# The queries' product between scores and sums, feed-forward products interleaved, and PSUM banks from a list

## The chip, the core and the metric

The kernel runs on one core of one Trainium2 chip. The metric is device microseconds of one execution. The core has TensorE (PE; its weight loads are shown apart as PEld), VectorE (DVE), ScalarE (ACT), GpSimd (POOL) and SyncE (SP), which issues the DMAs. TensorE writes to PSUM, 8 banks of 512 float32 per partition; VectorE and ScalarE read it from there.

## What is computed

A layer over `x` of shape (2, 256, 128, 128): batch, times T, bands FB, channels C. In float32, with 4 heads of 32 channels:

```python
xt = _ln(x, ln_t_w, ln_t_b).transpose(0, 2, 1, 3)
x = x + _mha(xt, t_wi, t_bi, t_wo, t_bo, H_T, causal mask over 256 times).transpose(0, 2, 1, 3)
xf = _ln(x, ln_f_w, ln_f_b)
x = x + _mha(xf, f_wi, f_bi, f_wo, f_bo, H_F, mask of the bands within 16 of each other)
xn = _ln(x, ln_n_w, ln_n_b)
h = gelu(xn @ w1.T + b1)          # 512 hidden channels
x = x + (h @ w2.T + b2)
```

`_mha` is attention: queries, keys and values from one product each, scores, softmax, weighted values, and an output product.

## The kernel before

**Groups.** The work is cut into 384 groups of 512 tokens (4 tiles of 128): 128 groups of attention over time (`OverTime`), and then, in 16 runs of 8 + 8, 128 groups of attention over bands (`OverBands`) and 128 of feed-forward (`FeedForward`). A run's 8 groups of bands are followed by the 8 feed-forward groups of the same tokens.

**The order is written out by hand.** `run` (line 1275) loops over n, and in iteration n it issues steps of several groups: the scores or first hidden products of group n, the sums of group n-1, the output of group n-2, queries, keys and values of group n+1, the normalization of group n+3. Every engine is wrapped by `InOrder` (line 897), so that each engine does its instructions in exactly that order. All recorded instructions therefore carry line 907, and groups are told apart by tile names.

**One group over bands, as TensorE meets it in iteration n** (8 groups of a run; when all neighbours are groups over bands):
- `first_half` / `scores` (775, 810): 64 matmuls from `qT`, `kT` into 4 banks, in 32x64 tiles of the array;
- `weigh` (814) of group n-1: the sums `rp` (`pf` by ones) and the weighted values `op` (`pf` by `v`), in 128x32 tiles;
- `output` (630) of group n-2: `wn` by `oT`;
- `queries_keys` (571) and `values` (590) of group n+1: `xnT` by `wf`, 128x32 tiles again. `product` (646) makes 4 matmuls, one for each 32 columns of the array; each stands as two records in the profile.

ScalarE in the same iteration: 4 exponentials (`first_function`, 790), `invert` (602) of group n-1, that is the logarithm `ln` of the sums and the exponential `r`, then the copies `qT`, `kT` and `v` of group n+1 out of PSUM.

VectorE: the band bias on the fourth head's scores (`bank<-bank,band`), `normalize` (441) of group n+3 (`xh`), `turn` (458), a transpose into `z`, `finish` (636) of group n-2, which adds the output product to the stream (`x<-bank`), `divide` (615) of group n-1 in three steps (`bank<-bank,r`, `u`, `oT`), and from the fifth group of a run on the statistics of a later group (`stats`, `mv`).

SyncE writes `z` to DRAM in four DMAs (`turned`), and `fetch` (470) reads the turned tile back as `xnT`, one iteration later, for the group two ahead of the iteration.

**One feed-forward group**: `first_half` (855) makes two of the four hidden products from `xnT`, `first_function` their gelus; then `weigh` (869) of group n-1 multiplies the hidden tile `hT` by `w2T` (16 products of 128 columns); then `second_half` and `second_function` the other two hidden products and gelus; `divide` (886) adds the result to the stream (`res`). In the first feed-forward group of a run (`turn`), the last group over bands is inverted by one VectorE `reciprocal` (`invert_exactly`, 610), and its output product comes at the end of the next iteration (line 1439).

**Banks.** `bank` (947) hands out PSUM banks: in the stage over time by fixed places, and in the other stages by counting round eight (`turn_of_bank`, 943); `follow` and `held` (line 817) set aside the turns of the output and of the next queries before the sums take theirs. A product into a bank waits until its last reader is done.

Of the kernel before, what the change touches and what calls it, by code (L numbers as in the profile page):

```python
# [19 lines left out]
P = 128  # L20
H = 4
# [4 lines left out]
NT = 4  # L26
# [343 lines left out]
class Group:  # L370
# [7 lines left out]
    def __init__(self, path, src, dst, before=None, store=None):  # L378
        self.path, self.src, self.dst = path, src, dst
        self.before, self.store = before, store  # L380

# [179 lines left out]
class Attention(Group):  # L561
    which = None
    swapped = ()
# [7 lines left out]
    def queries_keys(self):  # L571
        path = self.path
        wf = path.k.wf[self.which]
        self.qp = path.bank([P, NT * P], "qp", self.place.get("qp", path.held.pop("qp", None)))
        product(path, self.qp, wf[:, 0:P], self.xnT)

        self.kp = path.bank([P, NT * P], "kp", self.place.get("kp"))
        product(path, self.kp, wf[:, P : 2 * P], self.xnT)

    def take_query(self):  # L580
        path = self.path
        self.qT = path.work.tile([P, NT * P], F32, name="qT")
        path.scalar.activation(self.qT, self.qp, AF.Identity, bias=path.k.bq[self.which], scale=1.0)

    def take_key(self):
        path = self.path
        self.kT = path.work.tile([P, NT * P], F32, name="kT")
        path.scalar.copy(self.kT, self.kp)

    def values(self):  # L590
        path = self.path
        wv = path.k.wf[self.which][:, 2 * P : 3 * P]
        self.vp = path.bank([P, NT, P], "vp", self.place.get("vp"))
        for i in range(NT):
            product(path, self.vp[:, i], self.xnT[:, i * P : (i + 1) * P], wv, turn=2 if i in self.swapped else 0)

    def take_values(self):
        path = self.path
        self.v = path.work.tile([P, NT, P], F32, name="v", bufs=4)
        path.scalar.copy(self.v, self.vp)  # L600

# [13 lines left out]
    def divide(self):  # L615

        path, vector = self.path, self.path.vector
        if self.r0 is None:
            self.oT = path.work.tile([P, NT * P], F32, name="oT", bufs=2)
            u = path.work.tile([P, NT * P], F32, name="u", bufs=2)  # L620
            vector.tensor_tensor(by_rows(u), by_tile(self.op), by_tile(self.r), ALU.mult)
            vector.tensor_scalar(self.oT, u, -1.0, None, ALU.mult)
            return
# [4 lines left out]
        vector.tensor_tensor(by_rows(self.oT), by_tile(self.op), by_tile(u), ALU.mult)  # L628

    def output(self):  # L630
        path = self.path
        self.yp = path.bank([P, NT, P], "yp", self.place.get("yp", path.held.pop("yp", None)))
        for i in range(NT):
            product(path, self.yp[:, i], self.oT[:, i * P : (i + 1) * P], path.k.wn[self.which])

    def finish(self):
        self.path.vector.tensor_tensor(self.dst(), self.yp, self.dst(), ALU.add)
        if self.store is not None:
            self.store()
# [13 lines left out]
class OverTime(Attention):  # L653
# [7 lines left out]
    def values(self):  # L661
        path = self.path
        wv = path.k.wf[self.which][:, 2 * P : 3 * P]
        self.vp = [path.bank([P, 2, P], "vp", self.place.get(f"vp{s}")) for s in range(2)]
        for i in range(NT):
            product(
                path, self.vp[i // 2][:, i % 2], self.xnT[:, i * P : (i + 1) * P], wv, turn=2 if i in self.swapped else 0
            )

    def take_values(self):  # L670
        path = self.path
        self.v = path.work.tile([P, NT, P], F32, name="v", bufs=4)
        for s in range(2):
            path.scalar.copy(self.v[:, 2 * s : 2 * s + 2], self.vp[s])

    def first_tiles(self):
        path = self.path

        self.p0 = path.work.tile([P, 2, H, 2 * P], F32, name="p0", tag="p", bufs=3)
        self.s0 = {h: path.bank([P, 2, 2 * P], "sp", path.banks[f"a{h}"]) for h in range(H)}  # L680

    def second_tiles(self):
        path = self.path

        self.p1 = path.work.tile([P, 2, H, 2, P], F32, name="p1", tag="h", bufs=2)
        self.s1 = {h: path.bank([P, 2, P], "sp", path.banks[f"b{h}"]) for h in range(H)}
# [15 lines left out]
    def first_weights(self, heads):  # L702
        for h in heads:
            self.path.scalar.activation(self.p0[:, :, h], self.s0[h], AF.Exp)

    def second_weights(self, heads):
        for h in heads:
            self.path.scalar.activation(self.p1[:, :, h, 0], self.s1[h], AF.Exp)

# [17 lines left out]
    def weigh(self):  # L727
        path, v = self.path, self.v
        rp = path.bank([P, 2, 2, P], "rp", self.place.get("rp"))
# [4 lines left out]
        op = path.bank([P, 2, 2 * P], "op", self.place.get("op"))  # L734
# [33 lines left out]
class OverBands(Attention):  # L768
# [3 lines left out]
    follow = ("yp",)  # L772
    by_vector = 1

    def scores(self, heads):
        path = self.path
        self.sp = {h: path.bank([P, NT * P], "sp") for h in heads}
# [12 lines left out]
    def first_function(self):  # L790
        path = self.path
        for h in range(H - self.by_vector, H):
            sp = self.sp[h].rearrange("p (i q) -> p i q", i=NT)
            path.vector.scalar_tensor_tensor(
                sp, sp, LIMIT, path.band.unsqueeze(1).to_broadcast([P, NT, P]), ALU.min, ALU.add
            )
        for h in range(H):
            path.scalar.activation(self.p[:, h].rearrange("p i q -> p (i q)"), self.sp[h], AF.Exp)

# [14 lines left out]
    def weigh(self):  # L814
        path = self.path

        path.held = {name: path.turn_of_bank() for name in self.follow}
        self.rp = path.bank([P, NT * P], "rp")
# [5 lines left out]
        self.op = path.bank([P, NT * P], "op")  # L824
# [7 lines left out]
class FeedForward(Group):  # L832
# [8 lines left out]
    def hidden(self, js):  # L841
        path = self.path
        for j in js:
            self.hp[j] = path.bank([P, NT * P], "hp")
            product(path, self.hp[j], path.k.w1f[:, j * P : (j + 1) * P], self.xnT)

    def gelus(self, js):
        path = self.path
        for j in js:
# [3 lines left out]
            )  # L853

# [13 lines left out]

    def weigh(self):
        path, NI = self.path, self.path.k.NI  # L870
        if self.last:
            zp = [path.bank([P, P], "zp") for i in range(NT)]
        else:
            self.zp = path.bank([P, NT, P], "zp")
# [11 lines left out]
    def divide(self):  # L886
# [5 lines left out]
        else:  # L892
            self.path.vector.tensor_tensor(self.dst(), self.zp, self.dst(), ALU.add)
        self.store()
# [17 lines left out]
class BoundedPath:  # L912
    def __init__(self, ctx, tc, k):
# [6 lines left out]
        self.next_bank = 0  # L920
        self.inputs = 0
        self.held = {}
# [24 lines left out]
    def bank(self, shape, name, i=None):  # L947

        flat = self.ps[self.turn_of_bank() if i is None else i][:, 0 : math.prod(shape[1:])]
# [224 lines left out]
    def verdict(self):  # L1174

        vector, C = self.vector, P
        tp = self.bank([P, 6], "tp")
# [97 lines left out]
    def run(self, x, out):  # L1275
# [15 lines left out]
        for i in range(len(groups) - 2):  # L1291
            if at(i, OverBands) and at(i + 1, OverBands):
                groups[i].follow = ("yp", "qp")

# [18 lines left out]
        for n in range(len(groups) + 2):  # L1313
# [6 lines left out]
            if n + 4 in early:  # L1320
                do(n + 4, "root")
            do(n, "first_half", "first_function", "first_mask")
# [90 lines left out]
            if not turn:  # L1413
# [11 lines left out]
            do_at(n + 1, OverBands, "queries_keys", "take_query", "take_key")  # L1425
# [15 lines left out]
            do_at(n + 1, OverBands, "values", "take_values")  # L1441
            if old is not None or new is not None:
# [70 lines left out]
```

## Time and profile before

| | us |
|---|---|
| median of 3 runs | 2633.58 (2631.95 to 2634.81) |
| span of the profiled execution | 2631.9 |
| stage over time, to about | 930 |
| 16 runs of 8 + 8 groups, each about | 106 |

Busy time by engine, in stretches of the profiled execution (us; the count of instructions in brackets):

```profile
800.00:875.00 75.00, 75.00 (x2048) 52.20 (x2036) 63.56 (x188) 67.84 (x155) 69.31 (x65) 1.00 0.62 157
...
2000.00:2500.00 500.00, 499.81 (x13008) 362.56 (x13004) 411.17 (x1232) 301.79 (x496) 332.86 (x461) 1.00 0.49 123
```

The columns are the stretch, its length, the busy time of PE, PEld, DVE, ACT and POOL, then the granted TensorE clock (1.00 is full), the DMA engines' busy share and GB/s.

How to read a timeline row: start and length in us, engine, source line, operation, out<-in by tile names, the shapes (output<-inputs; for matmuls the tile of the array as rows*columns), how many instructions are merged in it, and in brackets the engine's idle time before it with what ended that. PEld rows are weight loads, which run beside matmuls. SPq rows are the issues of DMAs.

### The profile page before, as it was taken

The numbers are of one execution on the slowest core, as the hardware profiler recorded it, in microseconds if no ns is written. First come the engines' busy times: TensorE is split into PE (matmuls) and PEld (weight loads), VectorE is DVE, ScalarE is ACT, GpSimd is POOL, SyncE is SP. The second block draws the span as 40 slices with busy tenths as digits, with TensorE's granted clock in tenths as the row PEclk, the third lists the DMA queues.
The fourth block names the chain that finished last, engine by engine and source line by source line (L and its number), as shares of the span: only waits on it lengthen the run. The fifth ranks groups of instructions, "written<-read, shape, count | busy, mean of one in ns | idle before, by whom it ended". The sixth has DMA issues, their size and how long they took to land.

```text
span 2631.9 us, 156460 instructions
## 1 busy us (share of the span) xinstructions
PE 2617.8 (99%) x68688; PEld 1837.4 (70%) x68688; DVE 2140.8 (81%) x6410; ACT 1838.8 (70%) x3543; POOL 1958.6 (74%) x2311
## 2 busy tenths in 40 slices
PE   9999999999999999999999999999999999999999
PEld 6666666666766767666777776667676677777776
DVE  8888888888888887977878779788797797887974
ACT  7989988999899875564655746647557466475573
POOL 7999999999999987666667666665776666757762
PEclk9999999999999999999999999999999999999999
DMA  6656555565565454445454544554454445554543
GB/s 155 167 149 158 149 149 149 155 155 149 149 158 149 122 127 119 115 123 127 118 124 124 123 122 117 126 128 120 122 126 120 120 119 131 123 120 123 123 104 88
DMA packets 469797, 344.97 MB, mean 131 GB/s; under 512 B 43120, under 2 KB 404464, under 8 KB 469104
## 3 DMA queue, kind: packets, MB, share of 16 engines
q1 hardware_dynamic: 468408, 334.41, 50.5%
q8 instruction: 540, 8.85, 1.5%
q14 instruction: 153, 1.25, 0.2%
q10 hardware_dynamic: 696, 0.46, 0.1%
HBM read 167.98 MB, written 166.72 MB: 127 GB/s over the span
## 4 chain that ended last, share of the span: by engine, by line
PE 99%; DVE 0%; issue 0%; DMA 0%; ACT 0%; ACTq 0%; DVEq 0%
PE bank L907 99%; DMA x<-in_x 0%; DVE xh L907 0%; DVE bank L907 0%; DVE res L907 0%; DVE stats L907 0%; DVE oT L907 0%; DVE u L907 0%; DVE xnT L907 0%; ACTq L907 0%; ACT p L907 0%; DVE vy L907 0%; ACT lnv L907 0%; DVE mv L907 0%; ACT root L907 0%
## 5 line engine op out<-in xcount | busy, mean ns | idle before, releaser
L907 ACT ACTIVATE hT<-bank,b 128x512 f32<-128x512 f32 x512 | 348.1, 688 | 524.2 <-PE bank L907 483.2
L907 POOL TENSOR_SCALAR_AFFINE_SELECT pf<-pf 128x512 f32<-128x512 f32 x768 | 477.7, 637 | 185.3 <-ACT pf L907 159.1
L907 PEld LDWEIGHTS bank<-w2T_sb,hT 128*32 128x32 f32 x16384 | 467.4, 110 | 54.8 <-issue 29.0
L907 PE MATMUL bank<-xnT,wf 128*32 128x512 f32 x4096 | 492.4, 592 | 0.5 <-DVE xnT L907 0.5
L907 PE MATMUL bank<-xnT,w1f 128*32 128x512 f32 x4096 | 486.3, 592 | 0.2 <-issue 0.2
L907 PE MATMUL bank<-w2T_sb,hT 128*32 128x128 f32 x16384 | 482.8, 273 | 1.0 <-issue 1.0
L907 ACT ACTIVATE p<-bank 128x512 f32<-128x512 f32 (+1 forms) x1024 | 430.6, 494 | 62.9 <-PE bank L907 62.9
L907 DVE TENSOR_SCALAR xh<-x,mv,rstd 128x160 f32<-128x160 f32 (+1 forms) x1012 | 394.3, 432 | 59.7 <-POOL rstd L907 49.4
L907 POOL TENSOR_SCALAR_AFFINE_SELECT p<-p 128x1024 f32<-128x1024 f32 (+2 forms) x384 | 364.5, 949 | 57.5 <-ACT p L907 49.1
L907 PEld LDWEIGHTS bank<-wf,xnT 128*32 128x32 f32 x8192 | 243.3, 110 | 144.1 <-issue 101.6
L907 POOL TENSOR_TENSOR p<-p,p 128x512 f32<-128x512 f32 x256 | 324.6, 1291 | 10.6
L907 DVE BATCH_NORM_STATS2 stats<-x 128x6 f32<-128x128 f32 x1536 | 329.0, 276 | 3.4 <-DMA x<-in_x 3.4
L907 POOL TENSOR_SCALAR rstd<-mv 128x4 f32<-128x4 f32 x251 | 57.8, 230 | 361.7 <-DVE mv L907 360.5
L907 PEld LDWEIGHTS bank<-xnT,w1f 128*32 128x32 f32 x4096 | 183.6, 110 | 171.6 <-issue 109.6
L907 PE MATMUL bank<-qT,kT 32*64 32x80 f32 (+4 forms) x16384 | 302.0, 271 | 0.1
L907 PEld LDWEIGHTS bank<-qT,kT 32*64 32x64 f32 x16384 | 260.0, 131 | 51.2 <-ACT kT L907 50.6
L907 DVE TENSOR_TENSOR res<-bank,res 128x512 f32<-128x512 f32 (+1 forms) x259 | 170.3, 658 | 153.3 <-PE bank L907 144.7
L907 ACT ACTIVATE pf<-bank 128x512 f32<-128x512 f32 x512 | 265.8, 602 | 35.5 <-PE bank L907 31.3
L907 PE MATMUL bank<-wn,oT 128*32 128x128 f32 x8192 | 283.8, 274 | 0.1
L907 DVE STREAM_TRANSPOSE z<-xh 128x512 f32<-128x512 f32 x380 | 270.3, 711 | 13.3
L907 PE MATMUL bank<-wf,xnT 128*32 128x128 f32 x8192 | 276.5, 273 | 0.0
L907 POOL TENSOR_TENSOR rstd<-rstd,mhalf 128x4 f32<-128x4 f32 x251 | 260.8, 1039 | 20.9
(100 smaller groups left out, 3820.3 us busy)
## 6 DMA issues: line engine op xcount, KB each, us to landing
turned<-z SPq DMA_DIRECT2D x1520, 64.0 KB, 2.7
xnT<-turned SPq DMA_DIRECT2D x380, 256.0 KB, 3.2
x<-res SPq DMA_DIRECT2D x256, 128.0 KB, 2.5
x<-x SPq DMA_DIRECT2D x128, 256.0 KB, 4.1
out<-res SPq DMA_DIRECT2D x252, 128.0 KB, 2.3
x<-in_x SPq DMA_DIRECT2D x124, 256.0 KB, 4.3
x<-in_x SPq DMA_DIRECT2D x4, 128.0 KB, 2.8
x<-in_x SPq DMA_DIRECT2D x6, 64.0 KB, 2.9
```

The costliest lines, as they stand in the source:

```text
L907: return self.tc.keep_in_program_order(emit(*args, **kwargs))
```

## The change

1. `queries_keys` is split into `queries` and `keys`. Where groups n and n+1 are both over bands, the queries' product of group n+1 is issued between the scores of group n and the sums of group n-1, and its copy `take_query` behind `invert` (logarithm and `r`) of group n-1. Keys, their copy and values stay where they were. This concerns 7 of the 8 groups of a run.
2. Where groups n-1 and n are both feed-forward (7 iterations of a run), `weigh_around` issues tiles 0 and 1 of group n-1's second product, then hidden product 2 of group n, tiles 2 and 3, then hidden product 3. The gelus of products 2 and 3 follow.
3. Banks are taken from `free`, a list whose first entry has been free longest, and put back at its end once the last reader has been issued. In groups over bands that follow one another, the banks of sums and weighted values go back only at the end of the iteration (`keep`, `give_sums`). The stage over time keeps its fixed places.

```diff
+    def take(self, name, shape, i=None):
+        free = self.path.free
+        if i is None:
+            i = free[0]
+        if i in free:
+            free.remove(i)
+        self.taken[name] = i
+        return self.path.bank(shape, name, i)
+
+    def give(self, *names):
+        for name in names:
+            if name in self.taken:
+                self.path.release(self.taken.pop(name))
...
+    def weigh_around(self, other):
+        self.zp = self.take("zp", [P, NT, P])
+        self.weigh_tiles(range(0, 2))
+        other.hidden((2,))
+        self.weigh_tiles(range(2, NT))
+        other.hidden((3,))
...
-    def turn_of_bank(self):
-        i, self.next_bank = self.next_bank, (self.next_bank + 1) % 8
-        return i
...
+    def release(self, i):
+        if i in self.free:
+            self.free.remove(i)
+        self.free.append(i)
...
-            do(n - 1, "weigh")
+            if bands[2] and bands[3]:
+                do(n + 1, "queries")
+            if feeds[1] and feeds[2]:
+                groups[n - 1].weigh_around(groups[n])
+            else:
+                do(n - 1, "weigh")
             do(n - 1, "invert_exactly" if turn else "invert")
+            if bands[2] and bands[3]:
+                do(n + 1, "take_query")
             if new is not None:
                 new.first_weights(new.late)
             if bands[2] or turn:
                 do(n - 2, "output", "finish")
...
+            if bands[1] and bands[2]:
+                groups[n - 1].keep = True
             do(n - 1, "divide")
...
-            if not turn:
+            if feeds[1] and feeds[2]:
+                do(n, "second_function")
+            elif not turn:
                 do(n, "second_half", "second_function")
...
-            do_at(n + 1, OverBands, "queries_keys", "take_query", "take_key")
+            if bands[2] and bands[3]:
+                do(n + 1, "keys", "take_key")
+            else:
+                do_at(n + 1, OverBands, "queries_keys", "take_query", "take_key")
...
+            do_at(n - 1, OverBands, "give_sums")
```

`bands[i]` and `feeds[i]` tell whether group n-2+i is over bands or feed-forward, so `bands[2]` is group n itself.

More of the change, by code (lines that the diff above doesn't have):

```diff
@@ L569, in bias, with queries, keys, queries_keys @@
         )
-    def queries_keys(self):
+    def queries(self):
+        path = self.path
+        self.qp = self.take("qp", [P, NT * P], self.place.get("qp"))
+        product(path, self.qp, path.k.wf[self.which][:, 0:P], self.xnT)
+    def keys(self):
         path = self.path
         wf = path.k.wf[self.which]
-        self.qp = path.bank([P, NT * P], "qp", self.place.get("qp", path.held.pop("qp", None)))
-        product(path, self.qp, wf[:, 0:P], self.xnT)
-        self.kp = path.bank([P, NT * P], "kp", self.place.get("kp"))
+        self.kp = self.take("kp", [P, NT * P], self.place.get("kp"))
         product(path, self.kp, wf[:, P : 2 * P], self.xnT)
+    def queries_keys(self):
+        self.queries()
+        self.keys()
     def take_query(self):
@@ L592, in values @@
         wv = path.k.wf[self.which][:, 2 * P : 3 * P]
[L593 removed]
+        self.vp = self.take("vp", [P, NT, P], self.place.get("vp"))
         for i in range(NT):
@@ L628, in divide, with give_sums @@
         vector.tensor_tensor(by_rows(self.oT), by_tile(self.op), by_tile(u), ALU.mult)
+        if not self.keep:
+            self.give_sums()
+    def give_sums(self):
+        self.give("rp", "op")
     def output(self):
         path = self.path
-        self.yp = path.bank([P, NT, P], "yp", self.place.get("yp", path.held.pop("yp", None)))
+        self.yp = self.take("yp", [P, NT, P], self.place.get("yp"))
         for i in range(NT):
@@ L663, in values @@
         wv = path.k.wf[self.which][:, 2 * P : 3 * P]
-        self.vp = [path.bank([P, 2, P], "vp", self.place.get(f"vp{s}")) for s in range(2)]
+        self.vp = [self.take(f"vp{s}", [P, 2, P], self.place.get(f"vp{s}")) for s in range(2)]
         for i in range(NT):
@@ L679, in first_tiles @@
         self.p0 = path.work.tile([P, 2, H, 2 * P], F32, name="p0", tag="p", bufs=3)
-        self.s0 = {h: path.bank([P, 2, 2 * P], "sp", path.banks[f"a{h}"]) for h in range(H)}
+        self.s0 = {h: self.take(f"s0{h}", [P, 2, 2 * P], path.banks[f"a{h}"]) for h in range(H)}
     def second_tiles(self):
@@ L728, in weigh @@
         path, v = self.path, self.v
-        rp = path.bank([P, 2, 2, P], "rp", self.place.get("rp"))
+        rp = self.take("rp", [P, 2, 2, P], self.place.get("rp"))
         for n in range(2):
@@ L776, in scores @@
         path = self.path
-        self.sp = {h: path.bank([P, NT * P], "sp") for h in heads}
+        self.sp = {h: self.take(f"sp{h}", [P, NT * P]) for h in heads}
         for i in range(NT):
@@ L815, in weigh @@
         path = self.path
-        path.held = {name: path.turn_of_bank() for name in self.follow}
-        self.rp = path.bank([P, NT * P], "rp")
+        self.rp = self.take("rp", [P, NT * P])
         for h in range(H):
@@ L871, in weigh @@
         if self.last:
-            zp = [path.bank([P, P], "zp") for i in range(NT)]
+            zp = [self.take(f"zp{i}", [P, P]) for i in range(NT)]
         else:
-            self.zp = path.bank([P, NT, P], "zp")
+            self.zp = self.take("zp", [P, NT, P])
             zp = [self.zp[:, i] for i in range(NT)]
```

44 lines of the change are left out of this document (31 added, 13 removed).

## The prediction

> **What bounds the kernel now.** First the page: the span, the busy shares, the chain that ended last.
>
> ```profile
> span 2631.9 us, 156460 instructions
> PE 2617.8 (99%) x68688; PEld 1837.4 (70%) x68688; DVE 2140.8 (81%) x6410; ACT 1838.8 (70%) x3543; POOL 1958.6 (74%) x2311
> ...
> PE 99%; DVE 0%; issue 0%; DMA 0%; ACT 0%; ACTq 0%; DVEq 0%
> ```
>
> TensorE is busy all the way and the chain never leaves it. The ends of matmuls are modelled, so busy alone proves little. What settles it is whether matmuls start back to back, and that is read from the timeline by the distance from one start to the next. Here are TensorE's products in one group over bands, in the middle of a run of eight:
>
> ```profile
> 2432.03 0.97 PE L907 MATMUL bank<-qT,kT 32*64 32x80 f32 x64
> 2432.92 1.07 PE L907 MATMUL bank<-pf,ones 128*32 128x512 f32 x8
> 2433.80 1.06 PE L907 MATMUL bank<-pf,v 128*32 128x128 f32 x32
> 2434.68 1.06 PE L907 MATMUL bank<-wn,oT 128*32 128x128 f32 x32
> 2435.55 1.90 PE L907 MATMUL bank<-xnT,wf 128*32 128x512 f32 x16
> 2437.27 1.06 PE L907 MATMUL bank<-wf,xnT 128*32 128x128 f32 x32
> 2438.25 0.97 PE L907 MATMUL bank<-qT,kT 32*64 32x80 f32 x64
> ```
>
> From start to start: scores 0.89, sums 0.88, weighted values 0.88, output 0.87, queries and keys 1.72 (0.86 each), values 0.98, in all 6.22 us. The 32-column output and the values do the same work (32 matmuls of 128 columns), but values take 0.11 more because scores follow, in another tile shape. No product waits for data. So a reorder has almost nothing to win in such a group; what matters is whom the new order makes late.
>
> The engine nearest to being late is VectorE. Its timeline in the same place:
>
> ```profile
> 2433.18 0.70 DVE L907 SCALAR_TENSOR_TENSOR bank<-bank,band 128x512 f32<-128x512 f32 x1 [0.63 <-PE bank L907]
> ...
> 2435.42 0.71 DVE L907 STREAM_TRANSPOSE z<-xh 128x512 f32<-128x512 f32 x1
> 2436.06 0.65 DVE L907 TENSOR_TENSOR x<-bank,x 128x512 f32<-128x512 f32 x1
> 2436.64 0.69 DVE L907 TENSOR_TENSOR bank<-bank,r 128x512 f32<-128x512 f32 x1
> ...
> 2438.09 0.69 DVE L907 TENSOR_TENSOR oT<-bank,u 128x512 f32<-128x512 f32 x1
> 2438.69 0.86 DVE L907 BATCH_NORM_STATS2 stats<-x 128x6 f32<-128x128 f32 x4
> ...
> 2439.75 0.67 DVE L907 SCALAR_TENSOR_TENSOR bank<-bank,band 128x512 f32<-128x512 f32 x1
> ...
> 2446.29 0.67 DVE L907 SCALAR_TENSOR_TENSOR bank<-bank,band 128x512 f32<-128x512 f32 x1
> ...
> 2452.83 0.68 DVE L907 SCALAR_TENSOR_TENSOR bank<-bank,band 128x512 f32<-128x512 f32 x1
> ...
> 2458.32 0.69 DVE L907 SCALAR_TENSOR_TENSOR bank<-bank,band 128x512 f32<-128x512 f32 x1
> ```
>
> The row at 2433.18 (the fourth group's band bias) waited 0.63 for scores: VectorE still had time over. From the fifth group on it carries statistics too, and no later one of these rows shows idle time: they follow at 6.54 us (2439.75 to 2446.29 to 2452.83) where TensorE needs 6.22. VectorE falls behind by 0.3 a group. Where that lag ends is in the first feed-forward groups, where the last band group is inverted exactly:
>
> ```profile
> 2468.74 3.32 DVE L907 RECIPROCAL ln<-bank 128x512 f32<-128x512 f32 x1
> ...
> 2473.24 0.43 DVE L907 TENSOR_SCALAR oT<-u 128x512 f32<-128x512 f32 x1
> ```
> ```profile
> 2473.71 0.87 PEld L907 LDWEIGHTS bank<-wn,oT 128*32 128x32 f32 x30 [0.53 <-DVE oT L907]
> ```
> ```profile
> PEld bank L907 <- DVE oT L907: 9.9, 17, 0.8
> ```
>
> TensorE's output product of the last band group starts 0.04 after VectorE ends oT at 2473.67, and the table of waits counts 17 such: one for each of the 16 runs and one more. So at the end of every run it is VectorE's lag, not TensorE's own work, that says when TensorE goes on. What makes VectorE later between the fourth group and that point is paid in full, sixteen times.
>
> **The change part by part.** *Queries between scores and sums (7 of a run's 8 groups).* No instruction is added: TensorE's 6.22 us stay, and both neighbours have the sums' tile shape, so no switch is added. But sums, weighted values and the output product of two groups back each start 0.86 later. Behind the output product VectorE adds it to the stream (2436.06), and VectorE takes its work in program order: behind that add stand three steps of the division, the statistics and the next band bias. The output product now ends at 2435.55 + 0.86 = 2436.41. From the end of a product to VectorE's start the trace shows 0.26 (scores end at 2432.92, the band bias starts at 2433.18), so the add starts at 2436.67 instead of 2436.06: a new VectorE wait of 0.61. It arises in the third and in the fourth group. The third's is swallowed by the 0.63 that the fourth's band bias waits anyway; the fourth's is not, since nothing waits behind it any more. From the fifth group on VectorE's own lag hides the later product. So VectorE stands 0.6 later up to oT at 2473.24, and TensorE waits that much longer at 2473.71: 16 x 0.61 = 9.8 us. If VectorE had slack left there this would be 0; if the third group's wait passed through too, 19.5. I take 9.8, as the 0.63 is in the row.
>
> *Queries need their normalized input earlier.* The product moves ahead by sums, weighted values and output, 0.88 + 0.88 + 0.87 = 2.63 us. Its input comes by a DMA that SyncE issues when the transposed tile has landed.
>
> ```profile
> 2440.44 0.34 SPq L907 DMA_DIRECT2D xnT<-turned  x1
> ```
> ```profile
> DMA to landing us min/median/max: 2.6/3.2/4.9
> ```
> ```profile
> 1383.80 0.34 SPq L907 DMA_DIRECT2D xnT<-turned  x1
> ```
> ```profile
> 1386.07 1.06 PE L907 MATMUL bank<-pf,ones 128*32 128x512 f32 x8
> ...
> 1388.71 1.55 PE L907 MATMUL bank<-xnT,wf 128*32 128x512 f32 x12
> ```
>
> An ordinary fetch, issued at 2440.44 and landed by 2443.6 (median) or 2445.3 (worst), is wanted after the change behind the next group's scores, at 2438.25 + 6.22 + 0.89 = 2445.4: no wait, or just none. A late one, issued at 1383.80, is wanted at 1386.07 and lands at 1387.0 at the median, 1388.7 at worst: 0.9 to 2.6 of waiting. While TensorE waits there, sums and output stand behind it. Of the 16 runs a few have fetches like the second; my estimate from these rows is four late fetches a program of about 1 us, 4 us, with ends 0 and 9.
>
> *The queries' copy behind logarithm and reciprocal.* ScalarE's order is the same as before, only the copy's product is ready long before.
>
> ```profile
> 2454.66 0.63 ACT L907 ACTIVATE r<-ln 128x512 f32<-128x512 f32 x1
> 2455.48 0.69 ACT L907 ACTIVATE qT<-bank,bq 128x512 f32<-128x512 f32 x1 [0.19 <-PE bank L907]
> 2456.34 0.59 ACT L907 COPY kT<-bank 128x512 f32<-128x512 f32 x1 [0.17 <-PE bank L907]
> ```
> ```profile
> 2450.71 0.97 PE L907 MATMUL bank<-qT,kT 32*64 32x80 f32 x64
> ...
> 2457.09 0.97 PE L907 MATMUL bank<-qT,kT 32*64 32x80 f32 x64
> ```
>
> In the seventh group r ends at 2455.29, and the copies of queries and keys after it make scores late: 6.38 instead of 6.22. With the 0.19 before the queries' copy gone that is at most 0.16 a run, 2.6 us in all; but VectorE's extra 0.61 makes the exponentials, and so r, later again, and costs 0.2 to 0.5 there. Neither counts: TensorE catches up or not before 2473.71, where it waits for VectorE in any case. So 0, between -2.6 and +3.
>
> *Feed-forward products interleaved (7 of 8 groups).* Same products, same tile shape:
>
> ```profile
> L907 PE MATMUL bank<-xnT,w1f 128*32 128x512 f32 x4096 | 486.3, 592 | 0.2 <-issue 0.2
> L907 PE MATMUL bank<-w2T_sb,hT 128*32 128x128 f32 x16384 | 482.8, 273 | 1.0 <-issue 1.0
> ```
>
> Both stream 2,097,152 columns, and both take 483 to 486 us: a short product costs no more per column than a long one, so there is nothing to hide by mixing them. The Trainium skill ("TensorE: Matmul & The Clock Gate", back-to-back issue gap) says otherwise: about 81 ns for 128 columns and 131 ns for 512, that is, short products pay for their weight loads; by that rule mixing should gain. These rows do not show it here. The last gelu is covered by the next group's first two products (1.72 us against 0.69); the addition of the second product comes 0.86 later, on a VectorE that idles there once its lag is gone:
>
> ```profile
> 1547.49 0.69 DVE L907 TENSOR_TENSOR res<-bank,res 128x512 f32<-128x512 f32 x1 [2.02 <-PE bank L907]
> ```
>
> So 0; if the cover were missing, 0.86 in one group of a run, 14 us.
>
> *Banks by a list of freed ones.* Followed by hand, a list that gives the longest-freed bank gives in both stages the same distance as counting round eight. The tightest is scores on the bank of the output product: its add now ends near 2437.3 in the fourth group, scores start at 2438.25. So 0; up to 0.3 a group if VectorE's lag reaches it, which the 9.8 then contains.
>
> The sum: 9.8 + 4 = 13.8 on the profiled 2631.9 gives 2645.7. The profiled span is 1.7 below the median of the runs shown, 2633.6, so 2647.
>
> **Rivals.** *No change (24%).* VectorE's wait does not last: something in the 35 us between the fourth group and oT has slack that the timeline doesn't show, or the output product reaches VectorE sooner. For it: VectorE is busy only 81% over the span. Against it: the rows without idle time from 2439.75 on. Then 2633.6, down to 2631 with the seventh group's 2.6.
>
> *Faster (5%).* Weight loads do bound the short products. Then each group of the 112 interleaved ones has one more change from long to short, behind which one set of weight loads (110 ns, 467.4 us busy on the weight-load side over all short products) is hidden: 112 x 0.11 = 12.3, so 2621.
>
> ```profile
> L907 PEld LDWEIGHTS bank<-w2T_sb,hT 128*32 128x32 f32 x16384 | 467.4, 110 | 54.8 <-issue 29.0 <-ACT hT L907 10.9 <-ACT waste L907 0.3
> ```
>
> It decides from the point at which the first product behind a long one is cheaper than the others. The equal column rates speak against it. The Trainium skill's rule above (same page and section) is this mechanism stated for all kernels.
>
> *Slower still (7%).* The input is what binds: most of the 16 runs wait 1 us or more for a fetch, each wait holds back the output product and so VectorE again. 16 x (1 + 0.6) = 26 us, 2659. The decisive point is a fetch issued less than 3.2 us before the sums' old place.
>
> **How the numbers follow.** About 0.2% (5 us) can be told from no change. The forecast (64%) lies wholly above that, from +8 to +22. So slower 0.71, same 0.24, faster 0.05. The range 2631 to 2659 holds no change and the forecast with both its unknowns, and leaves out the faster rival and what is beyond the slower one. The forecast alone: 2641 to 2656.
>
> **What would show it.** In the changed timeline the add of the output should carry an idle time of about 0.6 before it in the third and fourth group of a run, ended by TensorE; the band biases after it should stand 0.6 further behind their scores; the wait of TensorE's weight loads for oT should grow from 9.9 to about 20 us. Some queries' products should start late behind scores, and the scores, feed-forward products and the stage over time should keep their distances. The prediction is wrong if the add shows no wait, or if it does and oT's wait doesn't grow.

## The result, and the profile after

| | us | against before |
|---|---|---|
| before, median of 6 runs beside it | 2633.94 (2631.95 to 2635.13) | |
| after, median of 6 runs | 2650.11 (2645.73 to 2660.39) | ratio 1.0066, 95% interval 1.0052 to 1.0079 |
| after, profiled execution | 2649.4, span 2646.7 | span 14.8 over before's 2631.9 |

The kernel became 16.2 us slower; 13.4 had been forecast. The page first: span, busy shares, and the chain that ended last.

```profile
span 2646.7 us, 156391 instructions
PE 2625.1 (99%) x68688; PEld 1872.6 (71%) x68688; DVE 2143.1 (81%) x6410; ACT 1835.2 (69%) x3543; POOL 1955.9 (74%) x2311
...
PE 92%; DMA 4%; DVE 3%; SPq 1%; issue 0%; ACT 0%; POOL 0%; ACTq 0%; DVEq 0%; POOLq 0%
```

Busy shares are as before; the chain is not. It had been TensorE for 99%, now 8% of it runs through DMA, VectorE and SyncE: TensorE waits for them in places.

Because all 16 runs of 8 + 8 groups are alike, the distance from one run's first scores to the next run's is the best measure in one trace. TensorE's timeline, before and after, the same run:

```profile
2413.32 0.96 PE L907 MATMUL bank<-qT,kT 32*64 32x80 f32 x64
...
2519.04 0.97 PE L907 MATMUL bank<-qT,kT 32*64 32x80 f32 x64
```
```profile
2426.60 0.97 PE L961 MATMUL bank<-qT,kT 32*64 32x80 f32 x64
...
2532.95 0.97 PE L961 MATMUL bank<-qT,kT 32*64 32x80 f32 x64
```

105.72 became 106.35. Of the 15 such distances in each trace, six before lie at 105.70 to 105.73 and seven after at 106.34 to 106.35: these are the undisturbed runs, and the change costs each of them 0.64 us. 16 x 0.64 = 10.2 of the 16.2. The other runs are longer by various amounts, in both kernels. Below, "shortest run" is that floor in a kernel's trace.

Where the 0.64 comes from is on VectorE. The additions of the output product (`x`) and the band biases, third to seventh group of that run:

```profile
2443.71 0.69 DVE L961 TENSOR_TENSOR x<-bank,x 128x512 f32<-128x512 f32 x1 [0.53 <-PE bank L961]
...
2446.39 0.70 DVE L961 SCALAR_TENSOR_TENSOR bank<-bank,band 128x512 f32<-128x512 f32 x1
...
2449.94 0.69 DVE L961 TENSOR_TENSOR x<-bank,x 128x512 f32<-128x512 f32 x1 [0.60 <-PE bank L961]
...
2453.66 0.67 DVE L961 SCALAR_TENSOR_TENSOR bank<-bank,band 128x512 f32<-128x512 f32 x1
...
2460.20 0.67 DVE L961 SCALAR_TENSOR_TENSOR bank<-bank,band 128x512 f32<-128x512 f32 x1
...
2466.74 0.67 DVE L961 SCALAR_TENSOR_TENSOR bank<-bank,band 128x512 f32<-128x512 f32 x1
```

The two additions in the third and fourth group wait 0.53 and 0.60 for TensorE; no later one does. The fourth group's band bias, idle for 0.63 before, has lost its slack. From there the biases follow at 6.54 as before, but each stands 0.63 further behind its scores.

Where TensorE pays for it is not where it was looked for. The table of waits, after, and the one row of it that is wanted of before:

```profile
DVE x L961 <- PE bank L961: 25.1, 36, 4.3
...
PEld bank L961 <- POOL pf L961: 15.7, 36, 0.9
...
PEld bank L961 <- DVE oT L961: 8.7, 16, 0.6
PE bank L961 <- DMA xnT<-turned: 8.5, 10, 1.9
```
```profile
PEld bank L907 <- POOL pf L907: 2.0, 8, 0.7
```

(Sum, count, longest.) VectorE's additions now wait 36 times, two a run and four more. The wait for `oT` has not grown from 9.9, it is 8.7. The wait for POOL's masks went from 2.0 to 15.7. POOL in the seventh group of a run, then TensorE's weight loads for the sums behind the eighth group's scores, after:

```profile
2573.55 0.23 POOL L961 TENSOR_SCALAR rstd<-mv 128x4 f32<-128x4 f32 x1 [1.29 <-DVE mv L961]
2573.86 1.04 POOL L961 TENSOR_TENSOR rstd<-rstd,mhalf 128x4 f32<-128x4 f32 x1
2574.87 5.22 POOL L961 TENSOR_SCALAR_AFFINE_SELECT pf<-pf 128x512 f32<-128x512 f32 x8
```
```profile
2578.85 0.11 PEld L961 LDWEIGHTS bank<-pf,ones 128*32 128x32 f32 x2 [0.88 <-POOL pf L961]
```
```profile
2558.72 0.23 POOL L907 TENSOR_SCALAR rstd<-mv 128x4 f32<-128x4 f32 x1 [1.28 <-DVE mv L907]
```

POOL works in order, and ahead of a group's six masks stands `rstd`, which needs VectorE's `mv`. The scores of these two groups start at 2570.62 (after) and 2556.43 (before): `rstd` starts 2.93 behind them now and 2.29 then, 0.64 later. The masks (0.65 each, 5.22 over 8) end 6 x 0.65 later, near 2578.8, and TensorE, which starts one half of those sums at 2577.83, starts the other half at 2578.85.

Those are rows of weight loads, and TensorE's own starts have to confirm them. A product is four matmuls, one for each 32 columns of the array. Their records start in pairs here, and one pair can run ahead of the other. The same sums in the run of 105.72, and after the change in that of 106.35:

```profile
2457.99 0.14 PEld L907 LDWEIGHTS bank<-pf,ones 128*32 128x32 f32 x4
2458.32 0.14 PEld L907 LDWEIGHTS bank<-pf,ones 128*32 128x32 f32 x4 [0.19 <-POOL pf L907]
```
```profile
2471.49 0.14 PEld L961 LDWEIGHTS bank<-pf,ones 128*32 128x32 f32 x4
2472.23 0.11 PEld L961 LDWEIGHTS bank<-pf,ones 128*32 128x32 f32 x2 [0.60 <-POOL pf L961]
```

In TensorE's single records, which merged rows hide, two matmuls start with the first load of each trace (2457.99, 2471.49) and the other two with the second (2458.33, 2472.23). The second pair starts when the last mask is done, and it did so before the change too: within 0.1 of the mask's end in 11 of the 16 runs, now in all 16. The table of waits (2.0 us before) hardly shows this: it counts idle time of all weight loading, 0.19 in the row above, where the second pair starts 0.33 behind the first. Behind the run's first scores this start moved from 45.00 to 45.63, and in both traces the next run's first scores follow 60.72 after it. So the 0.63 of this run is paid here, whole.

The second cost is the late input. SyncE's issue, the scores that the queries now follow, and the queries:

```profile
1693.11 0.34 SPq L961 DMA_DIRECT2D xnT<-turned  x1
```
```profile
1694.90 0.97 PE L961 MATMUL bank<-qT,kT 32*64 32x80 f32 x64
1697.81 1.83 PE L961 MATMUL bank<-xnT,wf 128*32 128x512 f32 x8 [1.94 <-DMA xnT<-turned]
...
2465.26 1.07 PE L961 MATMUL bank<-xnT,wf 128*32 128x512 f32 x8 [0.30 <-DMA xnT<-turned]
```

Ten such waits sum to 8.5 us. But not all count: the last row lies in the run of 106.35, one of the shortest. A wait of TensorE gives VectorE time, and the wait for the masks behind it shrinks.

### The profile page after: what moved, and what is told of

Its sections match the earlier page's. It is cut to its first block, busy times and chain, and to the rows that moved or that the text cites. A ratio compares the mean times of both kernels' runs of the same rounds, so it can differ in the third digit from the quotient of the medians.

```text
span 2646.7 us, 156391 instructions
## 1 busy us (share of the span) xinstructions
PE 2625.1 (99%) x68688; PEld 1872.6 (71%) x68688; DVE 2143.1 (81%) x6410; ACT 1835.2 (69%) x3543; POOL 1955.9 (74%) x2311
## 4 chain that ended last, share of the span: by engine, by line
PE 92%; DMA 4%; DVE 3%; SPq 1%; issue 0%; ACT 0%; POOL 0%; ACTq 0%; DVEq 0%; POOLq 0%
PE bank L961 92%; DMA xnT<-turned 2%; DMA turned<-z 1%; DVE xh L961 1%; SPq L961 1%; DVE stats L961 0%; DVE z L961 0%; DVE bank L961 0%; DVE x L961 0%; DVE u L961 0%; DVE oT L961 0%; DVE ln L961 0%; DVE mv L961 0%; DMA x<-in_x 0%; DVE res L961 0%
## 5 line engine op out<-in xcount | busy, mean ns | idle before, releaser
L961 PEld LDWEIGHTS bank<-w2T_sb,hT 128*32 128x32 f32 x16384 | 515.8, 110 | 87.8 <-issue 32.9
L961 PE MATMUL bank<-xnT,w1f 128*32 128x512 f32 x4096 | 544.8, 592 | 1.9 <-DVE ok L961 1.9
L961 PE MATMUL bank<-w2T_sb,hT 128*32 128x128 f32 x16384 | 532.5, 273 | 0.0
L961 PE MATMUL bank<-xnT,wf 128*32 128x512 f32 x4096 | 515.1, 596 | 9.2 <-DMA xnT<-turned 8.5
L961 PE MATMUL bank<-wn,oT 128*32 128x128 f32 x8192 | 289.3, 274 | 0.1
L961 DVE STREAM_TRANSPOSE z<-xh 128x512 f32<-128x512 f32 x380 | 270.5, 712 | 13.4
L961 PEld LDWEIGHTS bank<-xnT,w1f 128*32 128x32 f32 x4096 | 205.9, 110 | 106.6 <-issue 44.9
```

What stands on the lines that cost most here:

```text
L961: return self.tc.keep_in_program_order(emit(*args, **kwargs))
```

## The experiments

Besides time and ratio to the kernel before, the shortest run is given. Up to the eighth the edits are on the changed kernel.

**1. Queries back.**
```diff
-            if bands[2] and bands[3]:
-                do(n + 1, "queries")
...
-            if bands[2] and bands[3]:
-                do(n + 1, "take_query")
...
-            if bands[2] and bands[3]:
-                do(n + 1, "keys", "take_key")
-            else:
-                do_at(n + 1, OverBands, "queries_keys", "take_query", "take_key")
+            do_at(n + 1, OverBands, "queries_keys", "take_query", "take_key")
```


> The queries' product and its copy go back to the place of the keys, behind the output product; the interleaved feed-forward products and the list of banks stay. Theory (the queries' move is the whole loss: it makes VectorE's addition of the output product wait 0.6 us in the third and fourth group of each run, and it wants its input 2.6 us earlier): as before the change, 2634 us, no wait of TensorE for a transposed input, and POOL's masks again waited for by about 2 us in all instead of 15.7. Rival (the interleaving or the list of banks costs the time): stays near 2650. [...]

2635.39 us, ratio 1.0005 (0.9997 to 1.0014), shortest run 105.70, masks:

```profile
PEld bank L961 <- POOL pf L961: 2.5, 10, 0.9
```

The whole loss is gone, so interleaving and bank list together neither cost nor gain anything outside that interval. The prediction's rival had put the gain of mixing at 12.3 us, from the 110 ns of a weight load. The Trainium skill ("TensorE: Matmul & The Clock Gate", back-to-back issue gap) gives about 81 ns for 128 columns and 131 ns for 512, more per column for the short ones; no such gain shows in these runs.

**2. Queries moved, feed-forward products not interleaved.**
```diff
-            if feeds[1] and feeds[2]:
-                groups[n - 1].weigh_around(groups[n])
-            else:
-                do(n - 1, "weigh")
+            do(n - 1, "weigh")
```
(and the second half of the hidden products back at its old place)

> The queries' move and the list of banks stay; the feed-forward products are taken apart again as they were before the change. Theory (the queries' move is the whole loss): 2650 us, as the whole change, with the same waits for the transposed input (about 10 us) and for POOL's masks (about 16 us). Rival (the interleaving costs the time): 2634. If interleaving hides weight loads and so gains, this one is slower than the whole change: about 2662.

2649.37 us, ratio 1.0061 (1.0048 to 1.0074), shortest run 106.34: the queries' move alone is the whole change.

**3. The addition behind the division.**
```diff
-                do(n - 2, "output", "finish")
+                do(n - 2, "output")
...
             do(n - 1, "divide")
+            if bands[2]:
+                do_at(n - 2, OverBands, "wait_to_give", "finish")
```


> As the whole change, but in a group over bands VectorE divides (three steps, ready to start 0.3 us before the output product lands) ahead of adding the output product, whose bank is given back at the end of the iteration. Theory (VectorE's wait for the late output product is passed on): the wait of 0.6 becomes one of about 0.25 ahead of the division, the runs without a late input become 0.35 us shorter, 16 x 0.35 = 5.6: 2644.5 us, and the waits for POOL's masks fall from 15.7 to about 10. Rival (only the waits for the transposed input count, VectorE's lag costs nothing): 2650.

2646.37 us, ratio 1.0049 (1.0034 to 1.0063), shortest run 106.18: 0.16 won, not 0.35. Its band biases on VectorE, fourth to seventh group:

```profile
1267.11 0.70 DVE L970 SCALAR_TENSOR_TENSOR bank<-bank,band 128x512 f32<-128x512 f32 x1 [0.30 <-PE bank L970]
...
1274.01 0.67 DVE L970 SCALAR_TENSOR_TENSOR bank<-bank,band 128x512 f32<-128x512 f32 x1
...
1280.62 0.68 DVE L970 SCALAR_TENSOR_TENSOR bank<-bank,band 128x512 f32<-128x512 f32 x1
...
1287.23 0.67 DVE L970 SCALAR_TENSOR_TENSOR bank<-bank,band 128x512 f32<-128x512 f32 x1
```

0.30 of slack is back in the fourth group, as expected. But they now follow at 6.61, not 6.54, so VectorE loses half of it again in the three groups behind. The direction supports the theory; the size was missed.

**4. Queries behind the weighted values.**
```diff
-            if bands[2] and bands[3]:
-                do(n + 1, "queries")
             if feeds[1] and feeds[2]:
...
             do(n - 1, "invert_exactly" if turn else "invert")
             if bands[2] and bands[3]:
+                do(n + 1, "queries")
                 do(n + 1, "take_query")
```


> As the whole change, but the queries' product stands behind the weighted values instead of ahead of the sums; the output product keeps its later place. The input is wanted 1.75 us later, VectorE's addition waits as in the whole change. Theory (both the lag and the late input cost): the waits for the transposed input (about 10 us) nearly vanish, those for POOL's masks stay near 16; the 0.65 us a run that the runs without a late input lose stay, 16 x 0.65 = 10.4 above 2634: 2644 us. Rival (the late input is the whole loss): 2634. Other rival (the lag is the whole loss and the late inputs are covered by it): 2650.

2645.19 us, ratio 1.0043 (1.0030 to 1.0056), shortest run 106.33.

```profile
PEld bank L961 <- POOL pf L961: 11.7, 46, 1.0
...
PE bank L961 <- DMA xnT<-turned: 0.8, 1, 0.8
```

With the late inputs gone (8.5 to 0.8) the lag of 0.63 a run remains in full. 4.9 us is the price of the late inputs by these medians; the intervals just overlap.

**5. POOL's masks ahead of rstd.**
```diff
-            if n + 4 in early:
-                do(n + 4, "root")
...
             do(n, "first_half", "first_function", "first_mask")
+            if n + 4 in early:
+                do(n + 4, "root")
```


> As the whole change, but GpSimd raises the variance to its power (rstd, which waits for VectorE's late statistics) behind the masks of the iteration instead of ahead of them. Theory (the cause is VectorE's lag, and POOL only passes it on): the waits for POOL's masks fall from 15.7 us to 2 or less, but VectorE's lag then ends where the prediction had put it, and TensorE's waits for oT grow from 8.7 to about 18; the time hardly falls: 2648 us, an undisturbed run 106.2 to 106.35 us. Rival (GpSimd's place in the queue is itself the cause, and VectorE has slack up to oT): 16 x 0.64 = 10 us less, 2640, an undisturbed run 105.7, oT stays at 9.

2648.08 us, ratio 1.0047 (1.0034 to 1.0059), shortest run 106.17. Its waits, and the end of a run on VectorE and TensorE:

```profile
PEld bank L961 <- DVE oT L961: 19.5, 17, 1.6
...
PE bank L961 <- DVE oT L961: 5.0, 9, 0.7
PEld bank L961 <- POOL pf L961: 0.8, 3, 0.3
```
```profile
2485.83 0.43 DVE L961 TENSOR_SCALAR oT<-u 128x512 f32<-128x512 f32 x1
```
```profile
2486.31 1.08 PE L961 MATMUL bank<-wn,oT 128*32 128x128 f32 x32 [0.63 <-DVE oT L961]
```

The masks are no longer waited for, and the debt reappears where the prediction had put it: TensorE itself stands idle for 0.63 until `oT` ends. An undisturbed run costs 0.47 over before's 105.70 now, not 0.64 (experiment 8 shows why). The lag is VectorE's; POOL's queue only passes it on to TensorE some groups sooner.

**6 and 7. The move in some groups only.**
```diff
+            place = sum(all(at(n - j, OverBands) for j in range(i + 1)) for i in range(8))
+            moved = bands[2] and bands[3] and place not in (3, 4, 5)
...
-            if bands[2] and bands[3]:
+            if moved:
```
(in all three places; in 7 `place in (3, 4, 5)`)

> The queries' product is moved in the iterations of the first, second, sixth and seventh group of a run, and stands behind the output product, as before the change, in those of the third, fourth and fifth. Theory (only where VectorE has no backlog, in the third to fifth, does the late output product make it wait): no lag, an undisturbed run 105.7 us as before the change; the late inputs cost 4/7 of the 4.6 us that they cost net in the whole change: 2636.5 us, masks' waits about 2. Rival (each moved product costs its share, 4 of 7): 2634 + 16 x 4/7 = 2643.

2640.93 us, ratio 1.0022 (1.0013 to 1.0031), shortest run 105.72: no lag. But the time is 4.4 over what the theory gave and nearer to the rival's; its profiled execution has a span of 2635.0. TensorE's waits for late inputs sum to 3.7 in it, and those for the masks to 7.0 where about 2 had been expected. The lag's place is settled by this, the cost of the rest is not.

> The queries' product is moved in the iterations of the third, fourth and fifth group alone. Theory (VectorE's wait there is the whole lag): an undisturbed run 106.34 us as in the whole change, late inputs at 3/7: 2634 + 10.2 + 2 = 2646 us, masks' waits about 15. Rival (each moved product costs its share, 3 of 7): 2641.

2647.28 us, ratio 1.0047 (1.0035 to 1.0059), shortest run 106.36: the whole lag comes from these three groups.

**8. The sign in the ones** (on experiment 1).
```diff
-            vector.tensor_tensor(by_rows(u), by_tile(self.op), by_tile(self.r), ALU.mult)
-            vector.tensor_scalar(self.oT, u, -1.0, None, ALU.mult)
+            vector.tensor_tensor(by_rows(self.oT), by_tile(self.op), by_tile(self.r), ALU.mult)
...
+        return self.path.minus if self.final else self.path.k.ones[:, 0:D]
```


> The queries go back behind the output product, as in the first experiment; besides, for the last group over bands of a run the sums are taken with minus one in place of one, so that VectorE's separate change of sign (0.43 us, between u and oT) goes. Theory (at the end of every run TensorE waits for VectorE's oT, 9.4 us in all in the first experiment): each of the 16 waits of about 0.55 shrinks by 0.43 and the start of one instruction, so about 7 to 8 us less: 2627 us, an undisturbed run 105.25, oT's waits 2 or less. Rival (that wait is made good later in the run, by TensorE's next wait): 2634.

2633.93 us, ratio 0.9994 (0.9985 to 1.0003), shortest run 105.71: the rival's numbers.

```profile
PEld bank L964 <- DVE oT L964: 2.1, 7, 0.3
```

The waits shrank from experiment 1's 9.4 us to 2.1, and the time did not follow. TensorE's rows of before in that place:

```profile
2472.20 1.89 PE L907 MATMUL bank<-xnT,w1f 128*32 128x512 f32 x14
...
2473.71 1.14 PE L907 MATMUL bank<-wn,oT 128*32 128x128 f32 x30
```

Here too the single records run in two pairs. In each pair, records of 512 columns start 0.43 apart. The pair ahead starts its last one at 2473.16, would be free at 2473.59, and starts the output product at 2473.71: it waits 0.13 for `oT`, which ends at 2473.67. The pair behind starts its last one at 2473.49 and the output product at 2473.92, 0.43 later: it waits for nothing, and for it `oT` is some 0.2 early. It is the pair behind that the wait for the masks held back, and it sets the pace: in all 128 groups over bands of this trace the scores start 0.20 behind the last record of the values' product, whichever pair that is in. With the sign folded in, the pair ahead starts the output product 60.26 behind the run's first scores in place of experiment 1's 60.39, the pair behind at 60.59 in both, and the next run's scores come at 105.71 in both. So before the change VectorE had about 0.2 of slack at this place, and none at POOL's masks. That is why experiment 5, in which only `oT` collects, costs 0.47 and not 0.64.

**9. The output product ahead of the weighted values.**
```diff
+            three = bands[0] and bands[1] and bands[2]
+            if three:
+                do(n - 1, "sums")
+                do(n - 2, "output")
+                do(n - 1, "weigh_values")
...
+            if three:
+                do(n - 2, "finish")
```


> As the whole change, queries between scores and sums, but from the third group of a run on the output product stands behind the sums and ahead of the weighted values, so that it ends where it ended before the change; the weighted values, which only the third step of the division reads, are late instead. Theory (the late output product, and the wait of VectorE's addition for it, make the lag of 0.64 us a run): the addition starts 4.03 us behind the scores again, an undisturbed run is 105.55 to 105.7 us, the masks' waits are about 2, and the late inputs alone remain with about 10 us of waits and 4.6 net: 2638.5 us. Rival (sums or queries in their new places cost the time some other way): an undisturbed run stays at 106.34 and the time at 2650.

2638.49 us, the forecast time, ratio 1.0010 (1.0001 to 1.0019), but the shortest run is 105.84, 0.14 over the forecast, and the waits for masks sum to 8.8, not 2. The additions of the third and fourth group on VectorE have no idle time before them, and the fourth group's band bias between them has slack again:

```profile
2437.07 0.65 DVE L968 TENSOR_TENSOR x<-bank,x 128x512 f32<-128x512 f32 x1
...
2440.35 0.70 DVE L968 SCALAR_TENSOR_TENSOR bank<-bank,band 128x512 f32<-128x512 f32 x1 [0.49 <-PE bank L968]
...
2443.23 0.65 DVE L968 TENSOR_TENSOR x<-bank,x 128x512 f32<-128x512 f32 x1
```

The queries are still between scores and sums; with the output product back in time, 0.50 of the 0.64 are gone. So it was the late output product, not the queries' place as such, that made most of the lag. The other 0.14 stand at the masks: the sixth ends 45.07 behind the run's first scores here, 44.93 before the change and 45.57 after it.

**10. Output, then queries, then weighted values** (on 9; in a run's first two groups the queries stand as in 4).
```diff
                 do(n - 2, "output")
+                if bands[3]:
+                    do(n + 1, "queries")
                 do(n - 1, "weigh_values")
```


> From the third group of a run on: scores, sums, output, queries, weighted values, keys, values; in the first two groups the queries stand behind the second feed-forward product or the weighted values. So the queries' input is wanted 0.9 us earlier than before the change, not 2.6, the output product 0.9 earlier, and the queries' copy is still out of the way of logarithm and reciprocal. Theory: no lag, no late input, and the 0.16 us that the seventh group lost to late copies before the change are won: an undisturbed run 105.55, 2631.5 us, 2 or 3 less than before the change, which the measurement can hardly tell from none. Rival (the output product now comes before VectorE has its oT, which ends 1.15 to 1.3 us behind the scores where the product wants it at 1.78): 0.2 to 0.5 in several groups of a run, 2640 us or more.

2640.21 us, ratio 1.0015 (1.0006 to 1.0023), shortest run 105.84, not 105.55; no late inputs. The theory's number was missed by 9 us: the 0.16 of the seventh group was not won.

**11. The tenth, with the diffs of 5 and 8 added.**

> The order of the run before this one (output, queries, weighted values), and besides GpSimd's rstd behind the masks and the sign folded into the sums of a run's last group over bands. Theory (the three places through which VectorE's lag can reach TensorE then all have slack, and TensorE is back to back): an undisturbed run 105.5, 2631 us, no measurable difference from the run before this one. Rival (TensorE's products still wait for VectorE or POOL in a place that the waits for weights do not show): 105.2 or less, 2626.

2631.87 us, ratio 0.9987 (0.9978 to 0.9995), shortest run 105.35: the forecast number, but 0.49 under the run before it, where none was expected.

**12. Queries back (the diff of 1), with the diffs of 5 and 8 added.**

> The queries behind the output product as before the change (the interleaved feed-forward products and the list of banks stay), with the two changes of the run before: GpSimd's rstd behind the masks, and the sign folded into the sums of a run's last group over bands. Theory (in that run the earlier queries gave the seventh group's 0.16 us and the other two the rest): an undisturbed run 105.5 to 105.6 us, 2633 us, between the run before and the kernel before the change. Rival (the other two gave all of it): 105.35 and 2631.9, as the run before. Other rival (without the earlier queries nothing is gained, since TensorE is back to back): 105.7, 2634.5.

2629.90 us, ratio 0.9983 (0.9974 to 0.9992). Its first scores:

```profile
2406.53 0.97 PE L964 MATMUL bank<-qT,kT 32*64 32x80 f32 x64
...
2511.77 0.96 PE L964 MATMUL bank<-qT,kT 32*64 32x80 f32 x64
```

105.24, below all three forecasts. The time is 0.17% below the kernel before, just outside the interval, and the shortest run is below the eleventh's too. Both edits together give 0.46 a run. The sign alone gave nothing (8); masks first alone was run only with the queries moved (5: 0.17), so how much of the 0.46 is its own was not measured.

## Why the prediction was right, and where it was not

**Queries between scores and sums, 9.8 us: right in size and origin, wrong in its end.** The addition waits 0.60 in the fourth group (0.61 was worked out), the third group's wait is swallowed, VectorE carries the rest. Measured: 0.64 a run, 10.2 us. The step that failed is "VectorE stands 0.6 later up to oT at 2473.24, and TensorE waits that much longer at 2473.71". The prediction named its own test, that the wait for `oT` must grow, and it did not grow. The debt was collected earlier, through POOL: `mv`, `rstd`, masks, sums. Experiment 5 shows that it is one debt with two possible collectors. That the number came out all the same is luck: the masks, which the prediction does not mention, happened to have no slack, while `oT` had 0.2. With `oT` as the only collector, as in experiment 5, the term would have been 16 x 0.47 = 7.5 us.

**"At the end of every run it is VectorE's lag that says when TensorE goes on" was half a reading.** The rows were of weight loads. Of the output product's four matmuls two did wait for `oT`, 0.13; the two behind, which decide when the next scores start, did not (experiment 8). The rows quoted could not tell the two apart.

**"The copies of queries and keys after it make scores late: 6.38 instead of 6.22" names the wrong cause.** In that iteration, too, two of the sums' matmuls wait for a mask: the pairs start 38.28 and 38.45 behind the run's first scores before the change, 38.28 and 38.52 in experiment 10, and all four by 38.30 in experiment 12. The two that waited stay behind up to the values' product, and 0.20 behind its last record the next scores start: at 43.77 before, 43.84 in 10 and 43.61 in 12. (In the row quoted, too, the queries' copy waits 0.19 for TensorE, not for `r`.) So taking that copy out of the way, as 10 does, could not win the 0.16.

**Queries need their input earlier, 4 us (0 to 9): the waits were more than twice that, the net price is not settled.** Ten waits, 8.5 us, some of them absorbed. Removing them took 4.9 us off (4 against the whole change); but 10 has none, 9 has 6.4 us of them, and both have the same shortest run and 2640.2 against 2638.5 us. Between nothing and 5 is what can be said.

**Interleaving, 0; bank list, 0: as forecast** (1 and 2). The copy behind logarithm and reciprocal, also 0, was not tried apart from the queries' product. The rivals fall: no change and faster by the result, the input as the main cost by 4, where 0.63 a run remains without late inputs.

The traces also give the rest of the shortest runs. In the kernel before and after and in 1 to 4 and 6 to 10, the shortest run is the start of the second pair of those sums (44.99 before, 45.62 after, 45.46 in 3, 45.12 in 9 and 10) plus 60.72. With the masks first and `oT` early, in 12, no pair waits: all four start by 44.53, and the run is 105.24. Singly the edits of 5 and 8 leave the other collector in place.

What stays open: the net price of the late inputs, and with it what makes up the other 6 of the 16.2 us.

## What to carry to other kernels

When a product is moved ahead, ask which engine's in-order work stands behind the products that it pushes back, and whether that engine still has idle time there: a wait costs only where the last slack is used up. Then follow the lag through every queue that waits for that engine, since the first one without slack collects it, and that may be a third engine. A wait of weight loads is not a wait of TensorE until TensorE's own starts show a gap, and it must be a gap of those matmuls of a product that are behind: a merged row starts with the ones ahead.

## What the runs showed of the hardware

Two things were not expected. In experiment 3's order the same VectorE work took 6.61 us a group in place of 6.54; the three steps of the division then start 0.70 and 0.80 apart (1276.86, 1277.56, 1278.36) where they started 0.72 and 0.72 apart in the changed kernel (2457.09, 2457.81, 2458.53). And a product's four matmuls need not go in step, and can stay apart over many products. At a run's end values to scores takes 1.15 in the kernel before and 0.99 in experiment 12, and the copy of the keys starts 0.40 and 0.25 behind the first record of the values' product. Before, then experiment 12, TensorE and ScalarE:

```profile
2517.89 1.23 PE L907 MATMUL bank<-wf,xnT 128*32 128x128 f32 x32
...
2519.04 0.97 PE L907 MATMUL bank<-qT,kT 32*64 32x80 f32 x64
```
```profile
2518.29 0.59 ACT L907 COPY kT<-bank 128x512 f32<-128x512 f32 x1 [0.17 <-PE bank L907]
```
```profile
2510.78 1.06 PE L964 MATMUL bank<-wf,xnT 128*32 128x128 f32 x32
2511.77 0.96 PE L964 MATMUL bank<-qT,kT 32*64 32x80 f32 x64
```
```profile
2511.03 0.59 ACT L964 COPY kT<-bank 128x512 f32<-128x512 f32 x1 [0.17 <-PE bank L964]
```

The last records explain both. Those of the keys' product start at 2517.46 (two) and 2517.64 (two) before, and between 2510.35 and 2510.37 (all four) in experiment 12; the copy starts 0.64 and 0.66 behind the last of them, nearly the same. Those of the values' product start at 2518.84 and 2511.56, and the scores, in another tile shape, 0.20 behind in both, where one record of that product follows another on the same 32 columns after 0.11. So the first record of a product can stand some 0.2 ahead of what its reader waits for.
